# Attention statistics taken with each sum, closing ahead of the router's first part; transposed share first in a row's first output tile

## The chip, the cores and the metric

The kernel runs on one core of a Trainium2 chip. A core has five engines with queues of their own: TensorE (PE in the profile; its weight loads are PEld), VectorE (DVE), ScalarE (ACT), GpSimd (POOL) and SyncE (SP), which here only issues DMA transfers. Matmul results land in PSUM banks; everything else lives in SBUF or in DRAM. Engines wait for one another through semaphores, and each engine takes its own instructions in the order in which the program has them. The metric is the device time of one execution in microseconds (us); less is better.

## What is computed

Two layers. The first works on each of four images as a 128-channel matrix `q` of 4096 pixels, the second on 4096 tokens of 128 features per image. The reference, cut to what matters here:

```python
xs = x.reshape(B, C, h, R, w, R).transpose(0, 1, 3, 5, 2, 4).reshape(B, C * R * R, h, w)
q = xs.reshape(B, C * R * R, hw)
energy = jnp.einsum('bci,bcj->bij', q, q)
d = jnp.sqrt(jnp.diagonal(energy, axis1=1, axis2=2))
energy = energy / (d[:, :, None] * d[:, None, :])
attn = jax.nn.softmax(energy, axis=-1)
out = jnp.einsum('bcj,bij->bci', q, attn)
x = gamma * out + xs                        # back in the image's order
...
t = t + attention(_ln_t(t), Wk, Wq, Wv)     # linear: sums of Q (K^T V) over 8 heads
...
router_probs = softmax(_ln_t(t) @ router_w + router_b); top 2 of 8 experts
t = t + weighted sum of the two experts' products of _ln_t(t)
```

`_ln_t` subtracts a token's mean and divides by the root of its variance plus 1e-5.

## The kernel before, in words

**The first layer** (`attend`, from line 471). The pixels of an image are cut into eight chunks of 512. The pixel-by-pixel score matrix is symmetric, so only the tiles on and below one side of the diagonal are computed. A row `i` of output tiles goes through the chunks `jc` = 0 to `i`, and through four blocks `j` of 128 pixels in each. One such step does this: a score product `pe` (line 609, 128x512, from a pool of two PSUM banks), its exponential `pr` on ScalarE with a row sum (line 612), and, two steps later, the product `po` of that exponential with the pixels (line 497). `po` has one PSUM bank for the whole row. After its last product ScalarE evicts it to `o` (line 502), and only then may the next row's first `po` product start.

**The transposed share.** The other half of the symmetric matrix comes from the same exponentials. VectorE turns each `pr` in 32x32 blocks into `F` (line 421). SyncE writes `F` to DRAM (`blocks<-F`, line 530) and, three steps later, reads it back with the groups of partitions swapped, in six transfers (`F<-blocks`, line 545). The share, `transposed_share` (line 433), is then put into the list `late`. It is four products `pg`, each with a row sum on ScalarE (line 438), and at the end an addition to `o` on VectorE (line 442). The tile on the diagonal has a shorter form (`diagonal_share`, line 453). `step_share` takes one step of the first entry of `late` at the end of each step, once the entry's due time on the program's own clock has come.

**How work is delayed by steps.** `after(ticks, f)` keeps a call for so many steps later; `turn_tick` makes all calls that are due. So within a step the order on TensorE is: the score product, the `po` product of two steps ago, then a step of a transposed share.

**The second layer** (`layer1`) runs interleaved with the first layer of the next image: the main loop advances it by one `yield` after about every ten units of the program's clock, four units standing for one 128x512 product. `stagger` runs its four calls (`u` = 0 to 3, 1024 tokens each) overlapped, three advances apart. `attention_rows(u)` multiplies the turned rows with the attention matrix in three parts of 3, 3 and 2 row blocks (`pat`, line 855). Each part is evicted with an addition to the tokens `T` on VectorE (`add_rows`, line 920). Then come eight `bn_stats`, one for each row block (line 962), the closing of the statistics (`close_stats`), the router's first part (`router_rows`, four VectorE operations, lines 867 to 870), a copy of the new tokens to DRAM on SyncE's queue (`t2`, shown as `t<-T`, line 970), and the normalisation on ScalarE (line 696). `close_stats` is six small VectorE operations (lines 682 to 688) and then three on GpSimd: the power -1/2 (`rsf`, line 164), `nbf` (line 690) and `nbo` (line 692). The normalisation needs `rsf` and `nbo`. At odd `u` the routing and then the sorting of tokens by expert follow.

**Other queues.** On GpSimd stand, between those operations, indirect transfers that gather the experts' results of an earlier half (`acc<-ys`, line 1245); each waits for the exponential of its step. ScalarE issues the transfer that fetches the tokens for them (`acc<-t`, line 1233). SyncE also issues `blocks<-rows` (line 938, four transfers of small pieces for each `u`) and the results' stores (`out_dram<-acc`, line 1239). TensorE's, VectorE's, ScalarE's and SyncE's orders are those in which the program records the work; a scheduler places GpSimd's.

For the last image the second layer is run by `last_parts`, which the change does not touch.

## Time and profile before

| what | value |
|---|---|
| median of three timed runs | 1644.94 us (1643.99 to 1645.4) |
| the profiled execution's own time | 1638.94 us |
| span of its instructions | 1637.1 us |
| mean granted TensorE clock | 0.996 |
| VectorE's turns into F (line 421) | 440, mean 700 ns |
| ScalarE's normalisation (line 696) | 128, mean 495 ns |
| GpSimd's power for the router's statistics (line 164, rsf) | 15, mean 1751 ns |
| ScalarE idle until nbo was there | 20.7 us, 9 times, 3.8 us the longest |
| DMA traffic over the span | 213 GB/s of HBM traffic |

The span runs from the first to the last instruction of one profiled execution; the time of that execution has 1.8 us more around it. Times in a timeline count from the span's start. A row of a timeline gives start, length, engine, line, operation, output and inputs, shape and count, and in brackets how long the engine sat idle before it and what ended that. "PE ... x2" is a 32-bit product, which takes two passes.

### The profile page before, as it was taken

How to read it: one execution, taken by the hardware profiler on the slowest of the kernel's cores; microseconds unless marked ns; L12 is line 12 of the kernel's file. 1: busy time of each engine (PE TensorE's matmuls, PEld its weight loads, DVE VectorE, ACT ScalarE, POOL GpSimd, SP SyncE). 2: the span in 40 equal slices, each digit the busy share in tenths (PEclk: the TensorE clock that was granted, in tenths of full speed). 3: DMA queues.
4: the chain of work that ended last, by engine and by line, in shares of the span. 5: the costliest groups of instructions: out<-in, count | busy, mean ns of one | idle time of the engine just before them, and what ended most of it. 6: DMA issues, size and time to landing. Idle time of an engine off the chain costs nothing.

```text
span 1637.1 us, 20938 instructions
## 1 busy us (share of the span) xinstructions
PE 1598.4 (98%) x5075; PEld 832.8 (51%) x5075; DVE 942.7 (58%) x2383; ACT 877.2 (54%) x2779; POOL 593.8 (36%) x565
## 2 busy tenths in 40 slices
PE   8999999999999999999999999999999999999887
PEld 5444444455554455555554445555554445555633
DVE  5444353468487454449468545447758644344786
ACT  3555445456465544546555554556646554555386
POOL 1000000001024442446545553156555653437166
PEclk9999999999999999999999999999999999999999
DMA  4555656675759798997898889798798989886001
GB/s 139 199 193 174 202 179 213 236 231 179 171 206 269 238 230 248 255 263 206 208 221 270 263 214 277 216 281 222 203 212 256 298 238 257 252 254 192 15 14 39
DMA packets 364728, 345.18 MB, mean 211 GB/s; under 512 B 157504, under 2 KB 291136, under 8 KB 350272
## 3 DMA queue, kind: packets, MB, share of 16 engines
q1 hardware_dynamic: 330144, 304.33, 62.1%
q0 software_dynamic: 26624, 25.58, 7.7%
q10 hardware_dynamic: 7840, 13.93, 2.9%
q8 instruction: 43, 0.70, 0.2%
q14 instruction: 77, 0.63, 0.1%
HBM read 166.90 MB, written 182.09 MB: 213 GB/s over the span
## 4 chain that ended last, share of the span: by engine, by line
PE 84%; DVE 6%; DMA 4%; ACT 2%; issue 1%; POOL 1%; SPq 1%; ACTq 0%; DVEq 0%; POOLq 0%
PE po L497 25%; PE pe L609 24%; PE pg L433 21%; PE py L1371 3%; PE pg L453 2%; DMA F<-blocks 2%; PE pys L1180 2%; PE pys L1130 2%; PE pgram L725 2%; PE pat L855 1%; SPq L545 1%; DMA below<-F 1%; PE pys L1137 1%; ACT xn L696 1%; ACT pr L612 1%
## 5 line engine op out<-in xcount | busy, mean ns | idle before, releaser
L612 ACT ACTIVATE pr<-pe 128x512 f32<-128x512 f32 (+1 forms) x576 | 322.4, 560 | 614.5 <-PE pe L609 592.1
L497 PE MATMUL po<-pr,qT 128*128 128x512 f32 (+3 forms) x1152 | 549.8, 559 | 4.2 <-ACT o L502 3.5
L609 PE MATMUL pe<-qn,qn 128*128 128x512 f32 x896 | 460.4, 596 | 4.7 <-ACT pr L612 4.7
L433 PE MATMUL pg<-F,qT 128*128 128x512 f32 x880 | 450.4, 593 | 4.6 <-DMA F<-blocks 4.6
L421 DVE STREAM_TRANSPOSE F<-pr 128x512 f32<-128x512 f32 x440 | 305.1, 700 | 167.5 <-ACT pr L612 160.1
L497 PEld LDWEIGHTS po<-pr,qT 128*128 128x128 f32 x1152 | 215.6, 191 | 251.5 <-issue 219.4
L1245 POOL DMA_INDIRECT acc<-ys,place x128 | 202.1, 1579 | 210.4 <-ACT pr L612 135.0
L438 ACT ACTIVATE junk<-F 128x512 bf16<-128x512 f32 x440 | 273.1, 621 | 5.1 <-DMA F<-blocks 5.1
L433 PEld LDWEIGHTS pg<-F,qT 128*128 128x128 f32 x880 | 166.7, 190 | 199.5 <-issue 176.2
L1066 POOL DMA_INDIRECT xs<-xn,place x192 | 185.7, 967 | 176.3 <-ACT pr L612 109.8
L609 PEld LDWEIGHTS pe<-qn,qn 128*128 128x128 f32 x896 | 158.0, 191 | 131.4 <-issue 119.2
L442 DVE TENSOR_TENSOR o<-o,pg 128x512 f32<-128x512 f32 x110 | 75.2, 683 | 244.6 <-PE pg L433 244.4
L164 POOL TENSOR_TENSOR rn<-ss,neg_half 128x8 f32<-128x8 f32 (+1 forms) x17 | 27.2, 1603 | 321.0 <-DVE ss L296 320.9
L612 ACT ACTIVATION_READ_ACCUMULATOR pr<-pe 128x1 f32 x576 | 111.8, 194 | 0.0
L609 PE MATMUL pe<-qn 128*128 128x512 f32 (+3 forms) x256 | 91.5, 440 | 0.7 <-ACT qn L342 0.7
L1245 POOL DMA_INDIRECT yb<-ys,place x64 | 61.0, 953 | 77.8 <-DMA ys<-results 47.5
L438 ACT ACTIVATION_READ_ACCUMULATOR junk<-F 128x1 f32 x440 | 84.6, 192 | 0.0
L1112 DVE TENSOR_TENSOR results<-pys,xn 128x256 f32<-128x256 f32 (+1 forms) x60 | 24.9, 416 | 83.5 <-ACT xn L1106 70.4
L164 POOL TENSOR_TENSOR rsa<-dm_a,neg_half 128x8 f32<-128x8 f32 x16 | 28.9, 1807 | 104.7 <-DVE sv_a L688 104.6
L696 ACT ACTIVATE xn<-T,nbo,rsf 128x128 f32<-128x128 f32 x128 | 54.1, 495 | 20.7 <-POOL nbo L692 20.7
L1371 PE MATMUL py<-ew_sb,xn 128*128 128x512 f32 x128 | 60.2, 610 | 5.0 <-ACT tmp L1327 3.9
L164 POOL TENSOR_TENSOR rsf<-dm_f,neg_half 128x8 f32<-128x8 f32 (+1 forms) x15 | 26.3, 1751 | 105.2 <-DVE sv_f L688 105.2
(221 smaller groups left out, 1508.0 us busy)
## 6 DMA issues: line engine op xcount, KB each, us to landing
blocks<-F SPq DMA_DIRECT2D x110, 1024.0 KB
F<-blocks SPq DMA_DIRECT2D x220, 192.0 KB
F<-blocks SPq DMA_DIRECT2D x220, 128.0 KB
F<-blocks SPq DMA_DIRECT2D x220, 64.0 KB
below<-F SPq DMA_DIRECT2D x31, 384.0 KB
T<-in_x_dram SPq DMA_DIRECT2D x64, 128.0 KB
out_dram<-acc SPq DMA_DIRECT2D x128, 64.0 KB
xa<-in_x_dram SPq DMA_DIRECT2D x62, 128.0 KB
```

What stands on the lines that cost most here:

```text
L164: pinned(nc.gpsimd.tensor_tensor(dst, src, neg_half.to_broadcast(list(src.shape)), ALU.pow))
L421: f()
L433: nc.tensor.matmul(pg.rearrange("p (a f) -> p a f", a=4), st["qT"][i][:, ib, :], G[:, :, ib], start=(ib == 0), stop=(ib == NJ - 1),)
L438: nc.scalar.activation(junk, G[:, :, ib], AF.Copy, accum_out=st["sums"][:, NJ * i + ib, jc : jc + 1])
L442: nc.vector.tensor_tensor(st["o"][jc], st["o"][jc], pg, ALU.add)
L497: nc.tensor.matmul(row["po"][:, lo:hi], qT[blk // NJ][:, blk % NJ, :], w, start=start, stop=(row["left"] == 0))
L609: nc.tensor.matmul(pe[:, c0:], qn[jc][:, ts(j, P)], qn[i][:, c0:], start=True, stop=True)
L612: nc.scalar.activation(pr[:, c0:], pe[:, c0:], AF.Exp, accum_out=sums[:, t, i : i + 1]).ins
L696: nc.scalar.activation(xn[:, k, :D], T[:, k, :], AF.Identity, scale=rs[:, k, :], bias=nb[:, k, :])
L1066: inst = nc.gpsimd.indirect_dma_start(xs[h], offset(place[:, i, k : k + 1]), xn[:, k, :], None)
L1245: inst = nc.gpsimd.indirect_dma_start(to, None, ys, offset(place[:, i, k : k + 1]), compute_op=op)
L1371: nc.tensor.matmul(bank, xn[:, k, :D], ew_sb[:, 4 * h : 4 * h + 4, :], start=True, stop=True)
```

## The change

Two edits. In the first layer, a `po` product that comes due in the third step (`j == 2`) of a row's first tile is held back by `turn_tick` and called after `step_share`, so that a step of a transposed share, if one is due, stands ahead of it on TensorE. In the rows of the second layer, the `bn_stats` of each part's row blocks are taken right after that part's sum, `close_stats` follows directly, and the two yields that lay between the halves of the statistics come after it. The router's first part comes next, then the copy `t2`, which is now recorded in the same advance as the router's first part and not in the one after it; an additional `yield` after it keeps the normalisation where it was.

```diff
-    def after(ticks, f):
-        queued.append((tick[0] + ticks, f))
-
-    def turn_tick():
-
-        due = [f for at, f in queued if at <= tick[0]]
+    def after(ticks, f, can_wait=False):
+        queued.append((tick[0] + ticks, f, can_wait))
+
+    def turn_tick(starts=False):
+
+        due = [q for q in queued if q[0] <= tick[0]]
         queued[:] = [q for q in queued if q[0] > tick[0]]
-        for f in due:
-            f()
+        for _, f, can_wait in due:
+            if not (starts and can_wait):
+                f()
+        return [f for _, f, can_wait in due if starts and can_wait]
...
-                    after(2, partial(values, pr[:, c0:], t, c0, CH))
+                    after(2, partial(values, pr[:, c0:], t, c0, CH), True)
...
-                    turn_tick()
+                    left = turn_tick(jc == order[0] and j == 2)
                     clock[0] += 2 * (CH - c0) // P
                     step_share()
+                    for f in left:
+                        f()
                     yield
...
             la = stat.tile([P, 8, 2 * E], F32, tag="la", name=f"la_{b}_{u}")
+            bs, stats = batch_stats("f", 8 * u, 8)
             for j0 in range(0, 8, 3):
                 yield
                 pa, done = hold(f"pat_{b}_{u}_{j0}", partial(add_rows, u, j0, la))
                 attend_rows(u, j0, pa)
                 yield
                 done()
-            bs, stats = batch_stats("f", 8 * u, 8)
-            for j in range(8):
-                stats[j]()
-                if j == 3:
-                    yield
-                    yield
+                for f in stats[j0 : j0 + 3]:
+                    f()
+            close_stats("f", 8 * u, 8, bs)
+            yield
+            yield
             logits = router_rows(nc.vector, 8 * u, 8, la)
-            close_stats("f", 8 * u, 8, bs)
             next(logits)
-            yield
             nc.sync.dma_start(t2[:, ts(u, 8)], T[:, ts(u, 8), :])
+            yield
             yield
```

More of the change, by code (lines that the diff above doesn't have):

```diff
@@ L959, in attention_rows @@
                 done()
-            bs, stats = batch_stats("f", 8 * u, 8)
-            for j in range(8):
-                stats[j]()
-                if j == 3:
-                    yield
-                    yield
+                for f in stats[j0 : j0 + 3]:
[3 more added lines that the diff above has]
+            yield
             logits = router_rows(nc.vector, 8 * u, 8, la)
-            close_stats("f", 8 * u, 8, bs)
             next(logits)
+            nc.sync.dma_start(t2[:, ts(u, 8)], T[:, ts(u, 8), :])
             yield
-            nc.sync.dma_start(t2[:, ts(u, 8)], T[:, ts(u, 8), :])
             yield
```

## The prediction

> **What bounds the kernel now.** First the page's busy table, then TensorE's list of waits (engine line waited for: total us, times, longest).

> ```profile
> PE 1598.4 (98%) x5075; PEld 832.8 (51%) x5075; DVE 942.7 (58%) x2383; ACT 877.2 (54%) x2779; POOL 593.8 (36%) x565
> ```

> ```profile
> PE pe L609 <- ACT pr L612: 4.7, 3, 1.6
> PE pg L433 <- DMA F<-blocks: 4.6, 3, 2.3
> PE py L1371 <- ACT tmp L1327: 3.9, 4, 2.5
> PE po L497 <- ACT o L502: 3.5, 14, 0.5
> ```

> TensorE is the bound: no edit adds or removes a matmul, so the change can only win or lose TensorE's holes, and few us of those exist. The list understates them, because a matmul's modelled end runs past its successor's start. I therefore measure from start to next start: two passes of a 128x512 product repeat every 0.86 us. The change touches rows 1, 2 and 4.

> Row 1 is three holes, one in each of the first three images' row work, at the last of four calls of `attention_rows` (u=3). The timeline of the first (start, length, instruction, [idle before <- releaser]):

> ```profile
> 482.19 0.86 DVE L962 BATCH_NORM_STATS2 bs_f<-T 128x6 f32<-128x128 f32 x4
> ...
> 484.04 1.66 POOL L164 TENSOR_TENSOR rsf<-dm_f,neg_half 128x8 f32<-128x8 f32 x1 [8.26 <-DVE sv_f L688]
> ...
> 486.35 1.65 ACT L696 ACTIVATE xn<-T,nbo,rsf 128x128 f32<-128x128 f32 x4 [3.79 <-POOL nbo L692]
> ...
> 487.90 0.57 ACT L612 ACTIVATE pr<-pe 128x512 f32<-128x512 f32 x1
> ...
> 488.62 0.30 PEld L609 LDWEIGHTS pe<-qn,qn 128*128 128x128 f32 x2 [2.14 <-ACT pr L612]
> 488.62 1.13 PE L609 MATMUL pe<-qn,qn 128*128 128x512 f32 x2 [1.52 <-ACT pr L612]
> ```

> ScalarE sits 3.79 us in front of the normalisation until GpSimd has nbo; the exponential behind it comes late, and the score product, which has two banks, waits for that exponential. Its predecessor started at 486.29 and needs 0.65, so 1.68 us are lost here; the other two (875.38, 1259.99) lose 1.74 and 1.73 by the same subtraction: 5.15 us.

> Row 4 is the start of a row of output tiles. `po` has one bank; its first product waits for the eviction of the row before:

> ```profile
> 278.50 1.02 PE L609 MATMUL pe<-qn,qn 128*128 128x512 f32 x2
> 279.07 0.59 ACT L502 ACTIVATE o<-po 128x512 f32<-128x512 f32 x1
> 279.71 1.12 PE L497 MATMUL po<-pr,qT 128*128 128x512 f32 x2 [0.18 <-ACT o L502]
> ```

> Loss: 279.71 - 278.50 - 0.86 = 0.35 us. Going through all rows so, 14 with a transposed share next lose 0.35 and three (359.78, 740.94, 1127.70, the score product there is half as wide) 0.67: 4.8 + 2.0 = 6.8 us.

> Row 2 speaks against the change. TensorE, then SyncE's queue, at the worst hole:

> ```profile
> 844.85 1.02 PE L497 MATMUL po<-pr,qT 128*128 128x512 f32 x2
> 848.17 1.79 PE L433 MATMUL pg<-F,qT 128*128 128x512 f32 x2 [2.30 <-DMA F<-blocks]
> ```

> ```profile
> 832.03 5.10 SPq L938 DMA_DIRECT2D blocks<-rows  x4
> 837.23 7.54 SPq L545 DMA_DIRECT2D F<-blocks  x6
> 844.86 0.37 SPq L970 DMA_DIRECT2D t<-T  x1
> ```

> This share comes first in a row's first tile too; it waits for its transposed tile F, and today the first `po` product covers 0.86 us of the wait. The twin is at 1234.49.

> **Statistics and closing (attention_rows).** Nothing is added: eight bn_stats of 0.22 us (0.86 for four) and six closing operations (0.95 us) change place, in 12 calls. Six statistics now follow the first two sums, two the last. Before, between the last sum and the end of the closing stood four statistics, other work (at u=3 a turn of F, 0.7 us, and a part of the routing, 1.1 us), four statistics, the closing: 0.86 + 1.8 + 0.86 + 0.95 = 4.5 us. Now it is 0.44 + 0.95 = 1.4. The six earlier statistics delay the sum by up to 1.3 us only if VectorE is full; it is (16.14 of 17 us busy from 854 to 871), but there u=2 gives up the same six. So the sums ready GpSimd's power 1.8 to 3.1 us sooner. For the hole to vanish at 486 the exponential must end by 486.8, so the normalisation start by 484.6, 1.75 us sooner. It suffices, barely at the low end: gain between 1.5 x 3 and 5.15; I take 5.0.

> What moves with it: turns of F fall up to 1.9 us later (six statistics, and 0.5 from closing first), and SyncE's blocks<-F waits for them. The following tiles came with 2.7 us or more to spare, by the semaphores of their landings; cost 0, and beyond 2.7 us it would show. On GpSimd the power, which waits for VectorE, passes one indirect gather per image in two images; gathers then stand up to 4 us behind it, and the next have idle of 1 to 2 us before each to catch up: 0, at most 0.5 us. ScalarE's order is unchanged.

> **The t copy.** Its issue moves one step earlier and at u=0 passes, on SyncE, four blocks<-rows and the six F<-blocks of exactly the share that is late at 848 and 1234. Hardware transfers take eight completion semaphores in turn, and an issue waits for the last user. So the second of those six copies waited 4.6 us for `acc<-t`, which ScalarE issues at 838.13; that is the 7.54 above against 2.7 elsewhere. One transfer ahead shifts the turn: now the first of the six waits. All six, not five, are issued from 842.5 on: +0.47 us. The copy itself is 0.52 MB, at the 207 GB/s of the stretch from 820 to 835 2.5 us of a DMA system that is full there (share 1.08). [...] F lands 0.47 us later, between -0.5 and +3.

> **The share first.** 26 rows swap one share step with the first `po` product (where no share is due nothing moves). The share takes 0.86 us, the eviction is over by then: -6.8 us in all, if F is there. In two rows F lands 1.34 and 1.50 us ahead of the share's present start; the share starts 1.2 us sooner, just enough. In the two late rows the cover goes: behind the waiting share stand the `po` product, the `pat` products and the next score product. Each loses 0.86 + 0.47 = 1.33: +2.7 us (bounds +0.7 and +7.7).

> **The clock.** After the hole at 845 the granted clock is 0.50 for 3.41 us (848.44 to 851.86), in which the matmuls repeat at half rate: 1.77 us lost. The hole at 1232.6 (1.87 us, 1.53 of it in one such window) cost none. [...] By the row 2.3 us idle in one window was enough, 1.57 not; a hole of 3.2 lays over 2 us into one window in some four of five positions. The row decides: +1.8 us at the second place; at the first it is paid already.

> **Sum**: -5.0 - 6.8 + 2.7 + 1.8 = -7.3 us against the profiled execution: span 1637.1 to 1629.8, its time 1638.94 to 1631.6. The median of the timed runs, 1644.94, stands 6.0 above that execution; I carry the difference over: **1637.6 us**.

> **Rivals.**
> A, the late F costs less: acc<-t lands as early as now or earlier, the clock holds at the second place, so about -5.1 - 6.8 + 1.7 = -10.2: 1634.7. [...] 15%.
> B, VectorE is too full for the closing to come much sooner; the three holes shrink to two thirds (gain 1.5): 1641.1. For: 16.14 of 17 us; against: u=2 gives its share back. 12%.
> C, the t copy lies in front of acc<-t after all: F 3 us later at both places, -11.8 + 2 x 3.9 + 1.8 = -2.2: 1642.7. [...] 12%.
> D, slower: lateness of F spreads. Turned F later by 1.9, SyncE longer by the copy, F later by 5 us and more: then the late pairs lose 5.9 each, the next shares with 2.7 to 4.8 to spare wait 2 us each in both images, and two further windows run at half clock: -11.8 + 11.8 + 4 + 3.6 = +7.6: 1652.5. It decides from about 4 us of extra lateness. For: TensorE no longer has the `po` product as cover; against: each hole gives the following tiles their time back. 7%.
> The forecast itself: 54%.

> **How the numbers follow.** 0.2% is 3.3 us, about what a measurement of this kernel can tell from no change. The forecast and A lie clear on the faster side, B half, C mostly within: faster 0.76, within 0.17, slower 0.07. The range takes in A, the forecast with its bounds (A's 1633.5 to 1641) and most of C, and leaves out D: 1633.5 to 1643.

> **What would show it.** In TensorE's waits, pe on ACT pr falls from 4.7 to under 0.5, po on ACT o from 3.5 to under 0.5 (one early row has no share), pg on F<-blocks rises from 4.6 to about 7. ScalarE's wait for nbo falls from 20.7 us to under 8. The clock has two half-rate windows in mid-kernel. I am wrong if nbo comes no sooner, if shares in other rows wait for F, or if the late pair stands still.

## The result, and the profile after

| | before | after |
|---|---|---|
| median of the timed runs, same chip (22 each) | 1644.99 us | 1639.76 us |
| ratio after / before, 95% interval | | 0.9971, 0.996 to 0.9983 |
| span of the profiled execution | 1637.1 us | 1638.5 us |
| its granted clock | 0.996 | 0.995 |

The medians lie 5.2 us apart; by the ratio the change gains 0.29%, 2.8 to 6.6 us. Yet the span of the profiled execution is *longer* than before's. That contradiction turned out to matter: the two profiles were not taken under the same conditions (see the last fence of this section). First the lines that answer to those of before.

TensorE's waits after the change, and ScalarE's for `nbo` (line waited for: total us, times, longest):

```profile
PE pg L435 <- DMA F<-blocks: 8.7, 3, 3.7
PE py L1374 <- ACT tmp L1330: 3.9, 4, 2.5
PE pe L611 <- ACT pr L614: 3.3, 1, 3.3
...
PE po L499 <- ACT o L504: 0.2, 1, 0.2
```

```profile
ACT xn L700 <- POOL nbo L696: 6.9, 6, 1.8
```

`po` waits for an eviction once instead of 14 times, and ScalarE's wait for `nbo` fell from 20.7 us to 6.9. Both kinds of hole at which the change aimed are closed. `pg` waits 8.7 us for `F` where it waited 4.6, and one wait for an exponential is left that is as long as two of the old ones.

The first of the three `nbo` places, in the timeline after the change:

```profile
476.52 1.66 POOL L164 TENSOR_TENSOR rsf<-dm_f,neg_half 128x8 f32<-128x8 f32 x1 [7.67 <-DVE sv_f L692]
...
478.83 1.65 ACT L700 ACTIVATE xn<-T,nbo,rsf 128x128 f32<-128x128 f32 x4 [1.73 <-POOL nbo L696]
...
484.99 1.10 PE L611 MATMUL pe<-qn,qn 128*128 128x512 f32 x2
```

ScalarE idles 1.73 us in front of the normalisation instead of 3.79. The score product behind has no idle stretch in its bracket. A row's start:

```profile
275.49 1.02 PE L611 MATMUL pe<-qn,qn 128*128 128x512 f32 x2
276.06 0.59 ACT L504 ACTIVATE o<-po 128x512 f32<-128x512 f32 x1
276.35 1.02 PE L435 MATMUL pg<-F,qT 128*128 128x512 f32 x2
277.21 1.02 PE L499 MATMUL po<-pr,qT 128*128 128x512 f32 x2
```

275.49, 276.35, 277.21: three products 0.86 us apart, the eviction lying beside the share.

The first of the two late places, on TensorE and then on SyncE's queue:

```profile
835.26 1.02 PE L611 MATMUL pe<-qn,qn 128*128 128x512 f32 x2
839.98 2.05 PE L435 MATMUL pg<-F,qT 128*128 128x512 f32 x2 [3.69 <-DMA F<-blocks]
```

```profile
823.51 5.61 SPq L942 DMA_DIRECT2D blocks<-rows  x4
833.62 2.68 SPq L547 DMA_DIRECT2D F<-blocks  x6
```

SyncE is idle from 829.1 to 833.6; then all six copies go in one block of 2.68 us, behind `acc<-t`, which was issued at 829.40 and landed at 833.56 by the semaphore record. The first copy waits for semaphore 106, which `acc<-t` holds, until 833.58; the data that it reads, `blocks<-F`, had landed by 827.05. That is the turn of completion semaphores that the prediction described. In before's profile the fetch, issued with 106 at 838.13, landed at 842.54, and the second of the six copies, which carries 106 too, was issued at 842.55. In both profiles SyncE's 1634 transfers and ScalarE's 50 carry eight semaphores, 100 to 107. From one of SyncE's transfers to its next the number goes up by one (100 following 107) in 1586 of 1633 steps, by two in 45 and by three in 2; ScalarE's take the numbers between. The hole at 839.98 measures 3.86 us from start to start (predicted 2.46 + 1.33 = 3.79), the one at 1223.68 3.79 (predicted 3.36).

The clock, in stretches of one clock window each, 3.41 us by the last section (stretch: length, busy us of PE, PEld, DVE, ACT, POOL with counts, granted clock, DMA share, GB/s):

```profile
836.25:839.65 3.40, 0.04 (x1) 0.00 (x0) 2.40 (x8) 0.69 (x2) 2.63 (x2) 1.00 0.95 324
839.66:843.07 3.41, 3.09 (x4) 1.52 (x5) 0.00 (x0) 2.26 (x6) 0.00 (x0) 0.50 0.91 227
```

Half rate follows here, as before. At 1223 none followed in this execution; but one stands from 1310.69 to 1317.5 and one at 1512.08, where before had none. Those come from something else. The timeline:

```profile
1305.69 1.02 PE L611 MATMUL pe<-qn,qn 128*128 128x512 f32 x2
...
1310.97 0.60 ACT L614 ACTIVATE pr<-pe 128x512 f32<-128x512 f32 x1 [5.76 <-remote]
...
1311.71 2.08 PE L611 MATMUL pe<-qn,qn 128*128 128x512 f32 x2 [3.28 <-ACT pr L614]
```

The score product of 1305.69 was ready some 4 us before its exponential started, ScalarE had nothing else to do, and "remote" says that no event on this core's record ends the wait. This is no single event. From ScalarE's waits, first of after, then of before:

```profile
ACT pr L614 <- issue: 54.9, 44, 3.2
ACT pr L614 <- remote: 10.4, 2, 5.8
```

```profile
ACT pr L612 <- issue: 3.0, 2, 1.5
```

44 exponentials in one profile, and two in the other, follow an idle stretch for which the trace has no reason. The sum of ScalarE's idle time is hardly larger for it (762 us against 760; TensorE, busy for 97 and 98% of the span, is the bound), but in a few places the lateness reaches TensorE. So after's profile carries a disturbance that before's profile lacks, and their spans can't be subtracted.

### The profile page after: what moved, and what is told of

It is laid out like the page before. It is cut to its first block, busy times and chain, and to the rows that moved or that the text cites. A ratio compares the mean times of both kernels' runs of the same rounds, so it can differ in the third digit from the quotient of the medians.

```text
span 1638.5 us, 20936 instructions
## 1 busy us (share of the span) xinstructions
PE 1596.7 (97%) x5075; PEld 835.0 (51%) x5075; DVE 941.8 (57%) x2383; ACT 876.7 (54%) x2779; POOL 595.6 (36%) x565
## 4 chain that ended last, share of the span: by engine, by line
PE 87%; DVE 5%; DMA 3%; ACT 1%; issue 1%; SPq 1%; another core or an unknown queue 1%; POOL 1%; ACTq 0%; DVEq 0%; POOLq 0%
PE pe L611 26%; PE po L499 26%; PE pg L435 21%; PE py L1374 3%; PE pg L455 2%; PE pys L1183 2%; PE pys L1133 1%; PE pat L859 1%; PE pgram L729 1%; DVE df L762 1%; DMA F<-blocks 1%; DMA acc<-t 1%; PE pys L1140 1%; SPq L547 1%
## 5 line engine op out<-in xcount | busy, mean ns | idle before, releaser
L164 POOL TENSOR_TENSOR rn<-ss,neg_half 128x8 f32<-128x8 f32 (+1 forms) x17 | 27.2, 1603 | 316.7 <-DVE ss L296 316.6
L164 POOL TENSOR_TENSOR rsa<-dm_a,neg_half 128x8 f32<-128x8 f32 x16 | 28.9, 1808 | 103.8 <-DVE sv_a L692 103.6
L164 POOL TENSOR_TENSOR rsf<-dm_f,neg_half 128x8 f32<-128x8 f32 (+1 forms) x15 | 26.3, 1751 | 106.7 <-DVE sv_f L692 106.7
L611 PEld LDWEIGHTS pe<-qn 128*128 128x128 f32 x256 | 44.7, 191 | 36.8 <-issue 33.2
```

The source lines that it names most:

```text
L164: pinned(nc.gpsimd.tensor_tensor(dst, src, neg_half.to_broadcast(list(src.shape)), ALU.pow))
L611: nc.tensor.matmul(pe[:, c0:], qn[jc][:, ts(j, P)], qn[i][:, c0:], start=True, stop=True)
```

## The experiments

Each is the changed kernel with the edit shown, unless it says otherwise. They were run in three series on three chips; the kernel before took 1644.4, 1635.7 and 1636.3 us there. Ratios are to the kernel before on the same chip. Which chip the comparison of the first section ran on is not on record; with 1645.0 us for the kernel before it was like the first of these, and "the first chip" below means that of the first series.

**First series (before: 1644.36 us). The two edits apart.**

The held-back product alone, the rows of the second layer as before:

```diff
-                for f in stats[j0 : j0 + 3]:
-                    f()
-            close_stats("f", 8 * u, 8, bs)
...
+            for j in range(8):
+                stats[j]()
...
+            close_stats("f", 8 * u, 8, bs)
...
```

> The first edit alone; the second layer's rows as before. My theory (holes of TensorE add up): the 6.8 us at the row starts go, the two shares that wait for F lose the cover of one po product (0.86 us each; F itself lands as before), a second half-rate window may come (1.8 us); the three holes behind the normalisation stay. Net -3.3 to -5.1 us against before, po on ACT o under 0.5 us in TensorE's waits, pe on ACT pr still about 4.7. Rival (the row starts' 0.35 us are made up elsewhere anyway): within 1 us of before.

Measured: 1640.87 us, ratio 0.9983 (0.9972 to 0.9994). `po`'s waits for `o` are gone, the three holes at `nbo` stay at 1.69, 1.72 and 1.73 us. A new hole of 2.35 us stands at 1312.

The statistics alone, in the kernel before:

```diff
-                    left = turn_tick(jc == order[0] and j == 2)
+                    turn_tick()
...
-                    for f in left:
-                        f()
```

> The second edit alone; the first layer's order as before. My theory: the three holes behind the normalisation go (-5.0 us), the share at the fourth row start of images 3 and 4 waits 0.5 us longer each (+0.9, because the t copy moves the turn of the completion semaphores): net -4.1 us, pe on ACT pr under 0.5 us, po on ACT o still about 3.5. Rival (VectorE too full, closing hardly sooner): -1.5 us or less, with ScalarE's wait for nbo still over 12 us.

Measured: 1644.70 us, ratio 1.0002 (0.9986 to 1.0018). Its TensorE waits:

```profile
PE pg L433 <- DMA F<-blocks: 6.7, 3, 3.6
PE po L497 <- ACT o L502: 3.5, 14, 0.5
```

The three `nbo` holes (5.15 us) are closed, and the one wait for an exponential that is left (2.33 us at 1317) is at the place of the disturbance, but nothing was gained. At the two places where `F` is late 3.76 and 2.16 us are lost, 1.4 more than in before's profile, and half rate followed both, at 847 and at 1233; the granted clock's median fell by 0.001, 1.6 us. That is 3.0 of the 5.1 us; the other 2.1 were not placed, and lie within the ratio's interval (2.6 us either way). So neither theory held: the rival's sign, a wait for `nbo` of over 12 us, did not come (7.0), and the gain of the first was not seen in time.

The cover kept in the row in which `F` is late (images 3 and 4, row 4 keep the old order):

```diff
-                    left = turn_tick(jc == order[0] and j == 2)
+                    left = turn_tick(jc == order[0] and j == 2 and (b < 2 or i != 4))
```

> The changed kernel, but in the fifth row of output tiles of the third and fourth image, where the share waits for its F, the po product stands first again. My theory: the two holes shrink by 0.86 us each and the half-rate window behind them may go: 1.7 to 3.5 us faster than the changed kernel. Rival (what the shares lose is set by F's landing and given back by the next steps): no difference to the changed kernel.

Measured: 1638.53 us, ratio 0.9965 (0.9953 to 0.9977), 3.4 us below the changed kernel in the same series. The size fits, the reason only half: in the profile the hole at the first place fell to 3.02 us, but at the second it was 4.61, and both were followed by half rate. `F` itself landed later there: `acc<-t` took 5.2 us to land, 4.5 in the changed kernel's second profile. The granted clock of the timed runs has a median of 0.994, that of the changed kernel in this series 0.992; that alone is 3.3 us, so most of the gain came with fewer half-rate windows than this one profile shows.

The changed kernel again:

> The changed kernel once more, for a second profile. If the holes at 1308 and 1507 us of its first profile (3.4 and 2.5 us, each with half-rate windows behind it) belong to the change, they stand at the same places again; if they are accidents of one execution, they are gone and the span is about 10 us shorter. Time against before: -3 to -6 us as measured.

Measured: 1641.97 us, ratio 0.9984 (0.9973 to 0.9995). The mean granted clock of its runs has a median of 0.992, that of before's 0.996. Over 1640 us, 0.004 is 6.6 us. By an estimate from these figures the changed kernel runs some four half-rate windows more than the kernel before (3.41 us at a granted clock of 0.50 cost half of that, 1.7 us). Its profile has them at 839, 1222 (two in a row), 1314, 1512, 1539 and 1573.

All four profiles of this series show the disturbance of after's (46 to 53 idle stretches on ScalarE that nothing recorded ends; 51 in after's, 3 in before's).

**Second series (before: 1635.68 us).** First the kernel before once more, for its profile:

> The kernel before, unchanged, for a second profile. The profile of before has a span of 1637.1 us and no loss of TensorE time at the fourth image row's late tiles (around 1310 us) nor around 1510 us; all four profiles taken since (of the changed kernel twice, of each edit alone) have one at the first place (2.3 to 3.4 us) and half-rate windows behind it. Theory 1: the first profile of before was an undisturbed execution and these losses belong to both kernels: this one shows them too, span 1640 to 1645. Theory 2: the change brings them: none here, span within 1 us of 1637.1, at most one half-rate window in the middle (about 848).

Measured: span 1633.5 us, no loss at 1310, three idle stretches without a reason. That fits neither theory squarely, since this was a faster chip; no profile shows whether the kernel before meets the disturbance on the first one (its timed runs say more; see the part on the disturbance below).

The fetch on GpSimd's queue:

```diff
-                nc.scalar.dma_start(accs[g], t2[:, ts(g, 4)])
+                nc.gpsimd.dma_start(accs[g], t2[:, ts(g, 4)])
```

> The changed kernel with the fetch of the accumulators (acc<-t) issued from GpSimd's queue instead of ScalarE's. Theory 1 (the late F of the two row-8 stages is late because all six of its copies are issued behind the landing of the fetch, by a shared turn of completion semaphores): the copies are issued from about 830 and 1214 on without the wait of 4.1 us, F lands 3 to 4 us earlier, the waits of pg for F<-blocks fall from 3.9 and 3.8 us to under 0.5, and no half-rate window follows: 5 to 9 us faster than the changed kernel, 0.991 to 0.994 of before. Theory 2 (the copies wait for the work that feeds F, and the fetch only stands beside them): F lands when it did, ratio 0.996 to 0.998 as for the changed kernel. Theory 3: the issue costs GpSimd so much of the time in which it makes nbo that ScalarE's waits for nbo come back: slower than the changed kernel by 2 us or more.

Measured: **1620.12 us, ratio 0.9907** (0.9894 to 0.992). That is a little more than the first theory's 0.991 to 0.994. TensorE loses nothing at the two places. ScalarE's waits for `nbo` stay at 7.0 us, so the third theory falls.

The copy `t2` one advance later, as in the kernel before:

```diff
-            nc.sync.dma_start(t2[:, ts(u, 8)], T[:, ts(u, 8), :])
             yield
+            nc.sync.dma_start(t2[:, ts(u, 8)], T[:, ts(u, 8), :])
             yield
```

> The changed kernel with the copy t2<-T put back by one advance, to where it was issued before. By the turn of the completion semaphores the first of F's six copies then no longer waits for the fetch: five are issued behind it, as in the kernel with the first edit alone. Theory 1 (the term of 0.47 us per late F in the prediction): pg's wait at the two late places falls by about 0.45 us each, from 3.9 and 3.8 to about 3.4, together 0.9 to 1.9 us faster than the changed kernel. Theory 2 (t2's earlier place hides something else, the fetch itself starts later): the fetch lands later by one advance, some 1.3 us, and pg waits longer: 1 to 3 us slower.

Measured: 1626.98 us, ratio 0.9949 (0.9937 to 0.9962). SyncE's queue, with the first copy ahead of the wait again:

```profile
827.44 7.81 SPq L547 DMA_DIRECT2D F<-blocks  x6
```

Five copies wait, not six, as the turn of the semaphores wants it. The holes are 2.72 and 1.81 us; the changed kernel's, on the chip of the third series, 3.71 and 3.40. That is more than the 0.47 each of the prediction. In time the difference to the changed kernel (0.9962 there) lies within the intervals.

The fetch on GpSimd's queue in the kernel before (the same one line):

> The kernel before with the fetch alone moved to GpSimd's queue. Theory 1: the late F of before (2.5 and 2.0 us) goes, with its half-rate window (1.8): 4 to 7 us faster than before, 0.996 to 0.998. Then the fetch and the change add up, and the changed kernel with it stands another 6 to 7 us lower. Theory 2: F is late for another reason: ratio 1.000.

Measured: 1635.02 us, ratio 0.9995 (0.9988 to 1.0002): a miss. The two holes (1.49 and 1.80 us in the second profile of before) are gone, but no half-rate window stood behind them on this chip, so none could go; and in each kernel with the fetch on GpSimd the span ends 6.8 us after VectorE's last instruction, in the others 4.9. That takes back 1.9 us. The granted clock of its runs, 0.996 against 0.997, takes back another 1.6.

**Third series (before: 1636.29 us).** To have the changed kernel on such a chip too, beside the others:

> The changed kernel, unchanged. So far its comparison (0.9984) and those with the fetch or the copy moved (0.9907, 0.9949) stand on two chips, on which the kernel before takes 1644.4 and 1635.7 us: they cannot be subtracted. Theory 1 (what is lost is lost to the late F and the half-rate windows behind it, on either chip): ratio 0.9955 to 0.998; the kernel with the fetch on GpSimd in the same call is faster by at least 8 us. Theory 2 (the gain of 15.6 us seen with the fetch moved belongs to the chip): this kernel comes to 0.991 to 0.993 where before takes about 1636 us, and the fetch is worth less than 4 us beside it.

Measured: 1630.10 us, ratio 0.9962 (0.9949 to 0.9974).

> The kernel before, for a third profile, on the chip of this call. If before takes about 1644 us here: theory 1 (the losses near 1310 and 1510 us belong to this chip and to both kernels) a loss of 2 to 3.5 us at the fourth image row's late tiles and a span of 1640 to 1645; theory 2 (the change brings them there) none, and a span near 1637 with more than half of the timed runs near it. If before takes about 1636 us here: no such loss, as in the second profile (span 1633.5).

Measured: span 1634.4 us, no loss at 1310.

> The changed kernel with the fetch of the accumulators on GpSimd's queue, again, beside the changed kernel on one chip. Theory 1 (the fetch's turn of completion semaphores and the half-rate windows it brings are what the change lost): 0.990 to 0.992 of before on either chip, 8 to 14 us faster than the changed kernel; pg's waits for F<-blocks in the middle under 0.6 us, no half-rate window between 100 and 1500 us, and the end of the program 1.9 us longer after its last instruction (as with the fetch moved in the kernel before). Theory 2 (a matter of the chip): on the chip where before takes 1644 us the ratio is 0.995 or more.

Measured: 1621.89 us, ratio 0.9914 (0.9901 to 0.9927), 8.2 us below the changed kernel. TensorE's waits for `F`, first of the changed kernel, then with the fetch moved:

```profile
PE pg L435 <- DMA F<-blocks: 7.7, 3, 3.6
```

```profile
PE pg L435 <- DMA F<-blocks: 1.1, 1, 1.1
```

The one left is the first share of the kernel, at 181 us. By the two profiles the sum closes: holes of 3.71 and 3.40 gone, two windows at half rate gone (1.7 each), 1.9 us longer at the end: -8.6 against the measured -8.2. By the clocks of the timed runs (medians 0.995 and 0.996) it is one window rather than two, and -6.9. GpSimd and SyncE in the kernel with the fetch moved:

```profile
818.04 1.21 POOL L1236 DMA_DIRECT2D acc<-t  x1
```

```profile
820.14 4.63 SPq L942 DMA_DIRECT2D blocks<-rows  x4
824.87 2.96 SPq L547 DMA_DIRECT2D F<-blocks  x6
```

The copies now follow `blocks<-rows` after 0.1 us. The edit does two things at once, though: the fetch leaves ScalarE's queue, and the scheduler that places GpSimd's work issues it at 818.04, where the changed kernel had it at 828.78. Which of the two frees the copies was not separated by a run. By an estimate from the traces either would do alone: from GpSimd the fetch takes its semaphore from another set (112, of 111 to 118), for which none of SyncE's 660 copies into `F` waits in before's or after's profile, and issued at 818 it would have landed before 824.8 in any case, since it took 3.7 to 4.5 us to land in the changed kernel's three profiles.

The held-back product alone, with the fetch on GpSimd's queue:

> The first edit alone (the product held back behind the share), with the fetch on GpSimd's queue: with F on time the two edits can be priced without the windows. The two together with the fetch came to 14.9 us below before with the fetch (1620.1 and 1635.0). Theory 1 (the edits add up by the holes they close: 6.8 for the rows' starts, 5.1 for the statistics): about 7 to 8 us below before with the fetch, 0.9945 to 0.996 of before, with the three holes of ScalarE (1.7 us each) left. Theory 2 (they need each other): less than 4 us below, 0.997 or more.

Measured: 1625.97 us, ratio 0.9941 (0.9928 to 0.9954), with the three `nbo` holes at 1.72, 1.73 and 1.73 us. With `F` on time the edits can be priced: the statistics are worth 1625.97 - 1621.89 = 4.1 us. From the ratios 0.9995 and 0.9941, taken on two chips, the held-back product is worth 8.8 us. Both together gain 1635.02 - 1620.12 = 14.9 us within one series, 2.0 more than the two prices add up to, which were in part taken across chips.

## Why the prediction was right, and where it was off

**The direction and the range held**: 1639.76 us against 1637.6 in 1633.5 to 1643. The gain was forecast as 7.3 us and came out at 5.2 by the medians of the comparison, 2.4 in the first series and 6.2 in the third.

**The statistics and the closing** (-5.0) did in the trace what the prediction said: all three holes are gone in every profile with this edit, 5.1 us. In time the edit is worth 4.1 us where `F` is on time, and nothing measurable (1.0002) on the first chip. The sign named for it, TensorE's wait for exponentials under 0.5 us, failed in after's own profile (3.3 us, at the place of the disturbance) and came in every profile with both edits that lacks the disturbance.

**The share first** (-6.8): `po`'s losses behind `o` fall from 6.5 to 0.3 us in the third series' profiles. In time it gave 3.5 us on the first chip and 8.8 with `F` on time; the second figure is above the sum of its holes. The two profiles place the rest: their spans (1631.9 and 1624.1) differ by 7.8 us, and beside `po`'s holes the kernel with the product held back has one half-rate window less (1.7 us): one at 21 us, where the other has two, at 1528 and 1562. The granted clocks of the runs, 0.997 against 0.996, agree. None of the three follows a hole that the edit touches, so this part of the gain need not be the edit's.

**The late F** (+2.7): right in kind and place. The profile of after has 3.2 us more at the two places than before's; in the third series it is (3.71 + 3.40) - (1.48 + 1.14) = 4.5. The term was too small there because on such a chip `F` was less late before, while the changed kernel loses 3.4 to 4.1 us at each place in all its three profiles. The prediction's 0.47 us for one more copy behind the fetch is low too: with the copy `t2` put back the two holes shrink by about 1 and 1.6 us, as far as two chips can be compared. That the copy ahead of the fetch adds nothing of its own to the landing was the author's estimate, which no line of before shows. In the two profiles of the comparison the fetch landed 4.16 us after its issue with the copy ahead and 4.41 without.

**The clock** (+1.8) is the term that was sized worst. The prediction charged one window more, for a hole of 1.87 + 1.33 = 3.2 us at the second place, taking the one at the first place as paid already. In the third series before has none in the middle of the kernel and the changed kernel has both:

```profile
836.50:839.90 3.40, 0.69 (x2) 0.48 (x3) 2.12 (x7) 0.78 (x3) 2.46 (x2) 1.00 1.01 365
839.91:843.32 3.41, 3.41 (x5) 1.35 (x4) 0.00 (x0) 1.47 (x4) 0.00 (x0) 0.50 0.94 184
1218.80:1222.20 3.40, 0.66 (x2) 0.00 (x0) 3.02 (x9) 0.74 (x3) 3.06 (x2) 1.00 1.00 310
1222.20:1225.60 3.40, 2.90 (x4) 1.38 (x5) 0.00 (x0) 2.26 (x6) 0.15 (x1) 0.50 0.95 262
```

That is 3.4 us, and the medians of the granted clock say the same: 0.997 before, 0.995 after, 0.002 of 1630 us. On the first chip it is 0.004, 6.6 us. So the term is 3.4 to 6.6, not 1.8, which on the first chip turns the forecast 7.3 into 2.5, where 2.4 was measured. That so good an agreement came out is in part luck: some of those windows stand behind the holes of the disturbance, and the granted clock is recorded in steps of 0.001, 1.6 us each. On the chip of the third series the named terms come to -5.1 - 6.2 + 4.5 + 3.4 = -3.4 and the medians to -6.2; 2.8 us of gain stay unassigned. Between the two profiles, whose spans differ by 7.0 us, 1.7 of them are one half-rate window at the start and end that before's has more of; 1.9 stay open. A comparison at equal clock needs no such term: of the third series' runs at 0.995, four each, the kernel before took 1637.2 us and the changed kernel 1630.0, 7.2 less, and the holes alone come to -5.1 - 6.2 + 4.5 = -6.8. The prediction read one profile as if its windows were fixed. They were not: at the second place the hole of 3.79 us in after's profile, with at most 1.90 idle in one window (the last section), had no half rate behind it, and that of 3.40 us in the third series, with 2.74 idle in the stretch from 1218.80, had one window of it.

The row by which the prediction decided (2.3 us idle in one window, half rate in the next) was borne out: between 60 and 1480 us half rate followed every full-rate window with 1.99 us idle or more (the last section).

**The disturbance** was in no term, and could not be read from before's profile. In the five profiles that have it TensorE idles 2.0 to 3.3 us near 1310 us and 2.3 to 4.1 us near 1510, in four of them with half rate behind; the other nine profiles have neither hole. What holds ScalarE there no record shows. No profile shows whether it costs the kernel before as much, but that kernel's timed runs speak for it: those with a granted clock of 0.997 take 1642.7 us on the first chip (median of 12) and 1635.7 us on each of the other two (9 and 7 runs). At equal clock these 7.0 us are no half rate, and the disturbance's two holes come to 4.2 to 6.7 us. It would also explain the 6.0 us that the prediction carried over from the profile to the median without a cause: the profiled execution's 1638.94 us lies below all 22 timed runs of before in the comparison, the lowest of which took 1641.48. If so, carrying the difference over came out right by luck.

That the sum came out within 2.2 us of the measured median is luck in part too: the late `F` and the clock cost 2.1 to 6.6 us more than forecast, and in the third series 2.8 us of gain that no term had stand against them.

**The rivals.** A (late F costs less) falls: it costs more. B (VectorE too full) falls: no hole at `nbo` was left. C (the copy `t2` lies in front of the fetch) falls: `acc<-t` landed 4.16 us after its issue, and 4.41 before. D (lateness spreads) did not come: outside the late pair and the start of the kernel no share waits for `F`.

## What to carry to other kernels

Here the change took the cover off an operand that was already late and paid twice on TensorE: holes of 3.71 and 3.40 us in the third series, and behind each a window at half rate, 1.7 us; with the lateness removed the same two edits were worth 14.9 us, and 6.2 without, on two chips on which the kernel before takes nearly the same time. So look first for what makes the operand late (here a fetch on another queue, through a shared turn of completion semaphores) and move that, before or together with the reordering. And take a second profile of the kernel before: here one execution told neither which clock windows are typical nor whether it was an undisturbed one.

## What the runs showed of the hardware

```profile
1229.48:1232.89 3.41, 1.42 (x4) 0.68 (x4) 1.75 (x7) 1.25 (x6) 1.98 (x2) 1.00 0.97 356
1232.90:1236.31 3.41, 3.41 (x5) 1.35 (x4) 0.00 (x0) 3.06 (x9) 0.99 (x1) 0.50 0.92 180
```

```profile
1218.54:1221.95 3.41, 1.51 (x8) 0.68 (x6) 3.41 (x12) 1.59 (x5) 2.56 (x4) 1.00 0.91 237
1221.95:1225.36 3.41, 1.68 (x4) 0.87 (x5) 0.45 (x3) 1.65 (x5) 0.99 (x1) 1.00 1.02 343
```

In the second pair the hole is 3.63 us long, nearly twice that of the first, but the grid cuts it into 1.90 and 1.73. By an estimate from these figures, in this stretch of the kernel a hole under 1.9 us is free of the clock, one of 2 to 3.8 us is a matter of luck, and one of 4 us or more pays 1.7 us more wherever the grid cuts it, since a half of it is then 2 us.

Past 1480 us, where TensorE's work is a mix of shorter products, the border is not so sharp. There one window with 1.99 us idle (the statistics alone, from 1512.79) brought no half rate, and in nine profiles a window with 1.1 to 1.9 us idle, all of it in holes shorter than 0.9 us, did. With the fetch moved, third series:

```profile
1511.59:1515.00 3.41, 1.79 (x13) 1.15 (x11) 3.30 (x8) 0.70 (x2) 0.00 (x0) 1.00 0.00 0
1515.01:1518.42 3.41, 2.87 (x14) 2.88 (x15) 2.13 (x12) 0.48 (x1) 1.04 (x1) 0.50 0.00 0
```

What else counts there was not found.

**The three chips differed by more than the change.** The kernel before takes 1644.4, 1635.7 and 1636.3 us on three chips, in one series each; the change is worth 2.4 to 6.2. The idle stretches without a recorded reason fall on the same instructions wherever they occur: 14 of ScalarE's 2779 operations have one in all five profiles with the disturbance, four different kernels among them, and in none of the nine without. So it hangs on the place in the program as well as on the chip or the series.
